# A state space layer: two states per scan, with a zero-decay column between them

## The chip, the cores and the metric

The kernel runs on one core of a Trainium2 chip. The metric is device time in microseconds of one execution. A core has five engines with a queue each, which meet only at semaphores: TensorE (PE in the profile; its weight loads are PEld), VectorE (DVE), ScalarE (ACT), GpSimd (POOL) and SyncE (SP), which issues the transfers here. Data lies in SBUF, matmul results and some scratch in PSUM, which has eight banks of 512 fp32 values per partition.

## The reference

Two layers follow each other on an image x of 4 x 384 x 64 x 64, each with a group norm before it and a residual after it. The first is a state space layer over the 4096 positions of an image, with 768 inner channels and 16 states a channel; the second is a windowed attention with 7 x 7 windows. Only the first is touched by the change. Its core, with the projections before it left out:

```python
dt = jax.nn.softplus(jnp.einsum('blr,dr->bld', dt, dt_w) + dt_b)
A = -jnp.exp(A_log)
def step(h, inp):
    dt_t, B_t, C_t, x_t = inp
    dA = jnp.exp(dt_t[:, :, None] * A[None])
    dBx = (dt_t * x_t)[:, :, None] * B_t[:, None, :]
    h = dA * h + dBx
    y_t = jnp.einsum('bdn,bn->bd', h, C_t)
    return (h, y_t)
```

So for each channel d and state n there is a recurrence over positions, h = dA h + dt x B, and the output of a position is the sum over n of C h. Everything is fp32.

## The kernel before

An image's 4096 positions are cut into 16 chunks of T = 256; with four images this makes 64 steps. A step has 768 channels as 6 tiles of 128 partitions (index d), and the 16 states as 4 groups of 4 (index g). The pair (d, g) is numbered m = 4d + g, 0 to 23. Each m has two half groups of two states, so a step has 48 half groups. These are the kernel's clock: a plan lists for each of the 48 slots of a step what else is emitted there, and all engines run their queues in the order of emission.

For one m the work is:

- `decay` (ScalarE): for each of the two states of a half group, dA = exp(dt x A) over 256 positions, written to a PSUM tile `da` of one bank; two such tiles take turns. The decays of the next half group are emitted ahead of the scans of this one.
- `driven`: dt x B for four states at once, 1024 elements, written to an SBUF tile `db` (six in turn). For 9 of the 24 m's GpSimd does it, from `dtx` in SBUF; for 15 VectorE does it, from a copy of dtx in a PSUM bank of its own, `dtx_ps`. The table `driven_at` (L692) gives the slot and the engine.
- `dt_x` (GpSimd) makes dtx = dt times x once per d, and `dt_x_copied` (ScalarE) copies it to PSUM two slots later.
- `scans` (VectorE): the recurrence, one instruction per state over 256 positions, from `da`, `db` and a start value that is a pointer to the state kept from the chunk before (a constant 0 in an image's first chunk). The result goes to `hs` (five in turn).
- `with_c` (GpSimd): copies the last position of four states to `state`, then multiplies hs by C in place.
- `summed` (TensorE): eight transposing matmuls add the four states into PSUM; `turn` copies the sum out with ScalarE (`ys`), turns it back with TensorE and lets VectorE multiply by the gate.

Between these the plan places the work for the next steps: the projections and the convolution (TensorE, evicted by ScalarE with a bias), a burst of Silu activations with two table loads, the softplus in three parts (`softplus`: matmul, four Abs/Relu parts, Exp and an addition, Ln on ScalarE; three corrections on VectorE), the norm of the step after next, the output projection of the step before, and once per 24 slots statistics of the next image. Tiles of the pool `ps0` ("mm" in the profile), four PSUM banks in turn, hold all the matmul results.

The loads of B and C, broadcast to 128 partitions, and the image tiles are issued by SyncE. Semaphores are placed by a layer that follows tiles: an instruction waits for the earlier instructions that wrote or read the same tile or, in PSUM, the same tile's banks.

The line numbers in the profile are those of the kernel before. L96 is the helper through which all activations go.

Of the kernel before, what the change touches and what calls it, by code (L numbers as in the profile page):

```python
# [8 lines left out]
F32 = mybir.dt.float32  # L9
# [13 lines left out]
NG = 4  # L23
# [25 lines left out]
def two_layers(  # L49
# [151 lines left out]

    state = w0.tile([P, ND, NS], F32, name="state")
    xb = w0.tile([P, ND, KC - 1 + T], F32, name="xb")
# [67 lines left out]
    def layer0(x1s, mvs, gms1):  # L271

        with ExitStack() as es:
            es.enter_context(tc.manual_schedule(engines=in_step))
            ps_a = es.enter_context(tc.tile_pool(name="ps_a", bufs=2, space=PSUM))
            ps_x = es.enter_context(tc.tile_pool(name="ps_x", bufs=1, space=PSUM))
            ps_y = es.enter_context(tc.tile_pool(name="ps_y", bufs=1, space=PSUM))
            ps = es.enter_context(tc.tile_pool(name="ps0", bufs=4, space=PSUM))
            bc = es.enter_context(tc.tile_pool(name="bc", bufs=4))
            w1 = es.enter_context(tc.tile_pool(name="w1", bufs=1))  # L280
            w2 = es.enter_context(tc.tile_pool(name="w2", bufs=2))
            gms, gbs, st1s = {}, {}, {}
            dtx_ps = ps_x.tile([P, 2, T], F32, name="dtx_ps")

# [17 lines left out]
            def next_batch(b, at):  # L302
# [15 lines left out]
                for n in range(NJ * NXT):  # L318
                    t, j = divmod(n, NJ)
                    at(24 * n + 14, lambda t=t, j=j: load(t, j))  # L320
                    at(24 * n + 26, lambda t=t, j=j: nc.vector.bn_stats(st[:, j, t, :], h["x"]))
                end = 24 * NJ * NXT + 24
# [7 lines left out]
            def normed(I, h, at):  # L330
# [26 lines left out]
                def with_row(key, op):  # L357
                    nc.vector.tensor_tensor(
                        h["xn"], h["xn"], h[key][:, 0:1, :].broadcast_to([P, NJ, T]), op
                    )  # L360
# [10 lines left out]
                at(22, by_group)  # L371
                at(24, lambda: mean("xn", "mu"))
                at(26, lambda: with_row("mu", ALU.subtract))
                at(30, square)
                at(31, lambda: mean("sq", "var"))
                at(34, root)
                at(35, lambda: with_row("var", ALU.mult))

# [20 lines left out]
            def prepared(I, h, at):  # L399
# [21 lines left out]

                at(-11, kept)
                for p, (x, c, z) in enumerate((
                    ((-10, -9, -6), (1, 2, 5), (9, 10, 13)),
                    ((-6, -5, -2), (3, 4, 7), (12, 13, 16)),
                    ((-4, -3, 0), (7, 8, 11), (15, 16, 19)),
                )):
# [50 lines left out]

                at(26, burst)
                at(28, lambda: x_proj((0, 1, 2)))  # L480
                at(29, lambda: x_proj((3, 4, 5)))
                at(32, rows)

# [45 lines left out]

                for q, first in enumerate((34, 36, 46)):  # L530
                    softplus(q, first)

            dbs, das = {}, {}

# [7 lines left out]
            def dt_x_copied(d, h):  # L542
                nc.scalar.copy(dtx_ps[:, d % 2, :], h["dtx"][d])

            def driven(I, m, h, eng):

                d, g = divmod(m, NS // NG)
                db = w2.tile([P, NG, T], F32, tag="db", name=f"db_{I}_{m}", bufs=6)
                dtx = dtx_ps[:, d % 2, :] if eng is nc.vector else h["dtx"][d]
                eng.tensor_tensor(  # L550
                    db, dtx.unsqueeze(1).broadcast_to([P, NG, T]), h["B"][g], ALU.mult
                )
                dbs[I, m] = db

            def decay(I, m, half, h):

                d, g = divmod(m, NS // NG)
                da = ps_a.tile([P, 2, T], F32, tag="da", name="da")
                for k in range(2):
                    n = g * NG + 2 * half + k  # L560
                    act(da[:, k, :], h["dt"][d // 2][:, d % 2, :], AF.Exp, scale=nega[:, d, n : n + 1])
                das[I, m, half] = da

            def scans(I, m, half, hs):

                d, g = divmod(m, NS // NG)
                da = das.pop((I, m, half))
                for k in range(2):
                    j = 2 * half + k
                    n = g * NG + j  # L570
                    nc.vector.tensor_tensor_scan(  # L571
                        hs[:, j, :], da[:, k, :], dbs[I, m][:, j, :],
                        state[:, d, n : n + 1] if I % NCHUNK else 0.0,
                        ALU.mult, ALU.add,
                    )

            def with_c(I, m, h, hs):

                d, g = divmod(m, NS // NG)
                nc.gpsimd.tensor_copy(state[:, d, g * NG : (g + 1) * NG], hs[:, :, T - 1])  # L580
                nc.gpsimd.tensor_tensor(hs, hs, h["C"][g], ALU.mult)  # L581

            def summed(I, m, h, hs):
# [6 lines left out]
                for k in range(NG):  # L590
                    first = g == 0 and k == 0
                    last = g == NS // NG - 1 and k == NG - 1
                    for half in range(2):
                        nc.tensor.matmul(  # L594
                            y[:, d % 2, half, :], hs[:, k, half * P : (half + 1) * P], ident,
                            is_transpose=True, start=(first and half == 0 and d % 2 == 0),
                            stop=(last and half == 1 and d % 2 == 1), skip_group_check=True,
                        )

            def turn(I, p, h, at, s):  # L600

# [25 lines left out]
                at(s, out)  # L627
                at(s + 1, back)
                at(s + 4, gated)

            def out_proj(I, h, at):
# [37 lines left out]
                at(10, reload)  # L669
                for n, slot in enumerate((17, 18, 19, 20, 22, 23)):  # L670
                    m, part = divmod(n, 2)
                    at(slot, lambda m=m, part=part: tile_part(m, range(3 * part, 3 * part + 3)))
                at(26, lambda: residual(0, 2))
                at(28, lambda: residual(2, 1))
                at(30, stats)
# [8 lines left out]
            def slot_of(I):  # L684
# [9 lines left out]
                (12, 0), (15, 1), (17, 1), (18, 1), (20, 0), (22, 1), (24, 0), (26, 1),  # L694
                (26, 1), (26, 1), (30, 0), (33, 1), (36, 0), (39, 1), (40, 0), (43, 1),
            )
            dt_x_at = (-5, 2, 10, 18, 22, 34)

            for I in range(STEPS):
                h = steps[I]  # L700
                for p in range(ND // 2):
                    turn(I, p, h, slot_of(I), (p + 1) * (SLOTS // 3) + 4)
                out_proj(I, h, slot_of(I + 1))
# [5 lines left out]
                for m, (slot, vector) in enumerate(driven_at):  # L709
                    eng = nc.vector if vector else nc.gpsimd  # L710
                    slot_of(I)(slot, lambda I=I, m=m, h=h, eng=eng: driven(I, m, h, eng))
                if I % NCHUNK == 0 and I + NCHUNK < STEPS:
# [26 lines left out]
            for n in range(STEPS * M):  # L739
                I, m = divmod(n, M)  # L740
                hs = w2.tile([P, NG, T], F32, tag="hs", name=f"hs_{I}_{m}", bufs=5)
                for half in range(2):
# [422 lines left out]
```

## Time and profile before

| what | value |
|---|---|
| median of 7 runs | 8370.22 us (8360.2 to 8372.64) |
| the profiled execution's own time | 8370.22 us |
| its span in the profile | 8368.5 us |
| state space layer, first to last scan | 114 to 6021 us |
| attention layer | the rest, about 2300 us |
| VectorE / GpSimd / TensorE / ScalarE busy, whole span | 87 / 85 / 87 / 69% |
| the same from 2000 to 3000 us | 98 / 92 / 84 / 79% |
| granted TensorE clock there | 0.90 |

How to read it. A line of the groups of instructions names the source line, the engine, the operation, out<-in by the program's names, the shapes and the count; then, after the colon or bar, the busy time in us and the mean of one instruction in ns; then how long the engine had been idle before these instructions and which work ended most of that. A line of the timeline gives the start in us, the length in us, engine, line and operation, how many equal instructions follow each other (x4), and in brackets an idle time and what ended it. Instructions of one engine can overlap at their ends, so the distance between starts is what an instruction costs its engine.

### The profile page before, as it was taken

The numbers are of one execution on the slowest core, as the hardware profiler recorded it, in microseconds if no ns is written. First come the engines' busy times: TensorE is split into PE (matmuls) and PEld (weight loads), VectorE is DVE, ScalarE is ACT, GpSimd is POOL, SyncE is SP. The second block draws the span as 40 slices with busy tenths as digits, with TensorE's granted clock in tenths as the row PEclk, the third lists the DMA queues.
The fourth block names the chain that finished last, engine by engine and source line by source line (L and its number), as shares of the span: only waits on it lengthen the run. The fifth ranks groups of instructions, "written<-read, shape, count | busy, mean of one in ns | idle before, by whom it ended". The sixth has DMA issues, their size and how long they took to land. (4 is left out here: it accounts for less than half of the span.)

```text
span 8368.5 us, 139186 instructions
## 1 busy us (share of the span) xinstructions
PE 7250.8 (87%) x45882; PEld 5492.5 (66%) x45882; DVE 7312.5 (87%) x13300; ACT 5810.4 (69%) x13758; POOL 7092.7 (85%) x5719
## 2 busy tenths in 40 slices
PE   7888888888888888888888888888699999999999
PEld 5676677777667667676777677766555555555555
DVE  5999999999999999999999999999766666666666
ACT  5777777777777777777777777777545455455455
POOL 4999999999999999999999999999767677677677
PEclk9988898889888998999899889889799999999999
DMA  3112211121122112211211121112223233233232
GB/s 112 59 61 66 75 58 54 64 72 58 63 67 71 53 60 68 69 58 65 71 59 54 57 70 55 54 61 66 70 85 87 75 96 88 75 92 85 84 86 65
DMA packets 327504, 583.06 MB, mean 70 GB/s; under 512 B 62940, under 2 KB 211180, under 8 KB 326660
## 3 DMA queue, kind: packets, MB, share of 16 engines
q1 hardware_dynamic: 326788, 574.17, 22.1%
q8 instruction: 370, 6.06, 0.3%
q14 instruction: 346, 2.83, 0.1%
HBM read 471.49 MB, written 84.73 MB: 66 GB/s over the span
## 5 line engine op out<-in xcount | busy, mean ns | idle before, releaser
L571 DVE TENSOR_TENSOR_SCAN hs<-da,state,db 128x256 f32<-128x256 f32 x5760 | 3856.5, 729 | 88.8 <-ACT da L96 64.6
L96 ACT ACTIVATE da<-dt,nega 128x256 f32<-128x256 f32 x6144 | 2918.0, 477 | 1211.4 <-DVE hs L571 1105.3
L581 POOL TENSOR_TENSOR hs<-hs,C 128x1024 f32<-128x1024 f32 x1536 | 3621.5, 2358 | 123.9 <-POOL state L580 0.4
L594 PE MATMUL y<-ident,hs 128*128 128x128 f32 x12288 | 1773.3, 296 | 910.0 <-POOL hs L581 907.7
L594 PEld LDWEIGHTS y<-ident,hs 128*128 128x128 f32 x12288 | 1538.0, 153 | 1213.2 <-POOL hs L581 1107.2
L941 POOL TENSOR_SCALAR sg<-sg,rsum 128x308 f32<-128x308 f32 x1536 | 1619.9, 1073 | 643.8 <-DVE rsum L939 641.8
L550 POOL TENSOR_TENSOR db<-dtx,B 128x1024 f32<-128x1024 f32 x576 | 1360.2, 2361 | 0.1
L550 DVE TENSOR_TENSOR db<-dtx_ps,B 128x1024 f32<-128x1024 f32 x960 | 1142.5, 1201 | 0.0
L382 PE MATMUL mm_ps<-xn,w_in 128*128 128x256 f32 x4608 | 1125.2, 391 | 11.0 <-DVE yg L624 9.1
L96 ACT ACTIVATE sg<-sg,mx 128x308 f32<-128x308 f32 x1536 | 828.6, 541 | 252.0 <-DVE mx L926 232.9
L926 DVE CUSTOM_DVE_ANT_0 sg<-lg_ps,bias 128x308 f32<-128x308 f32 x1536 | 643.1, 475 | 384.8 <-PE lg_ps L920 384.8
L382 PEld LDWEIGHTS mm_ps<-xn,w_in 128*128 128x128 f32 x4608 | 872.6, 197 | 119.9 <-DVE yg L624 9.6
L389 PE MATMUL mm_ps<-xb,dcv 128*128 128x256 f32 x3072 | 782.3, 408 | 0.0
L389 PEld LDWEIGHTS mm_ps<-xb,dcv 128*128 128x128 f32 x3072 | 616.2, 208 | 87.6 <-issue 0.3
L969 ACT COPY tb<-pt_ps 88x512 f32<-88x512 f32 x384 | 221.8, 578 | 625.1 <-PE pt_ps L965 625.1
L580 POOL COPY state<-hs 128x4 f32<-128x4 f32 x1536 | 288.6, 188 | 342.5 <-DVE hs L571 336.0
L639 PE MATMUL mm_ps<-yg,w_out 128*128 128x256 f32 x2304 | 538.1, 384 | 0.0
L956 DVE COPY ta<-pt_ps 110x512 f32<-110x512 f32 x768 | 492.4, 683 | 23.2 <-PE pt_ps L951 23.2
L639 PEld LDWEIGHTS mm_ps<-yg,w_out 128*128 128x128 f32 x2304 | 437.9, 194 | 58.1
L951 PE MATMUL pt_ps<-ident,sg 128*110 128x128 f32 x3072 | 417.7, 279 | 0.8 <-POOL sg L941 0.8
L951 PEld LDWEIGHTS pt_ps<-ident,sg 128*110 128x110 f32 x3072 | 322.7, 133 | 77.9 <-issue 48.4
L824 PE MATMUL mm_ps<-xn,w_qkv 128*128 128x512 f32 (+2 forms) x612 | 279.9, 595 | 60.4 <-DVE xn L811 53.2
(141 smaller groups left out, 9148.2 us busy)
## 6 DMA issues: line engine op xcount, KB each, us to landing
B<-bcrows SPq DMA_DIRECT2D x256, 512.0 KB
C<-bcrows SPq DMA_DIRECT2D x256, 512.0 KB
vw<-vd SPq DMA_DIRECT2D x1792, 33.0 KB
xr<-x SPq DMA_DIRECT2D x28, 1056.0 KB
vd<-v SPq DMA_DIRECT2D x280, 96.0 KB
xi<-in_x_dram SPq DMA_DIRECT2D x64, 384.0 KB
xo<-in_x_dram SPq DMA_DIRECT2D x64, 384.0 KB
x<-xo SPq DMA_DIRECT2D x64, 384.0 KB
```

What stands on the lines that cost most here:

```text
L96: ins = nc.scalar.activation(o, i, func, **kw)
L382: nc.tensor.matmul(pb[:, k, :], w_in[:, j, m * P : (m + 1) * P], xn[:, j, :], start=(j == 0), stop=(j == NJ - 1),)
L389: nc.tensor.matmul(pb[:, k, :], dcv[:, d, c, :], xb[:, d, c : c + T], start=(c == 0), stop=(c == KC - 1),)
L550: eng.tensor_tensor(db, dtx.unsqueeze(1).broadcast_to([P, NG, T]), h["B"][g], ALU.mult)
L571: nc.vector.tensor_tensor_scan(hs[:, j, :], da[:, k, :], dbs[I, m][:, j, :], state[:, d, n : n + 1] if I % NCHUNK else 0.0, ALU.mult, ALU.add,
L581: nc.gpsimd.tensor_tensor(hs, hs, h["C"][g], ALU.mult)
L594: nc.tensor.matmul(y[:, d % 2, half, :], hs[:, k, half * P : (half + 1) * P], ident, is_transpose=True, start=(first and half == 0 and d % ...
L639: nc.tensor.matmul(h["po", first][:, m - first, :], w_out[:, d, m * P : (m + 1) * P], h["yg"][d // 2][:, d % 2, :], start=(d == 0), stop=( ...
L926: nc.vector.tensor_tensor_reduce(sg[:, hh, :], lg[:, :NK], bias[:, 4 * m + hh, :], -1.0, BIG, ALU.add, ALU.min, mx[:, hh : hh + 1],)
L941: nc.gpsimd.tensor_scalar(sg[:, hh, :], sg[:, hh, :], rs[:, hh : hh + 1], None, ALU.mult)
L951: nc.tensor.transpose(pt[: KN[c], col : col + P], sg[:, 2 * pair + hh, KOFF[c] : KOFF[c] + KN[c]], ident,)
L956: nc.vector.tensor_copy(t[: KN[0], :, :].rearrange("p a q -> p (a q)"), pt[: KN[0], :])
```

## The change

Two states share one scan. The scan runs over 513 elements: 256 positions of the first state, one column, 256 positions of the second. In the column the decay is 0 and the addend is the second state's kept value, so that the recurrence arrives at exactly that value there, whatever the first state ended with, and goes on with the second state. A step has 48 scans in place of 96.

What goes with it:

- `da` and `dtx_ps` become two PSUM tiles `pair_0` and `pair_1` of 1024 values, two banks each. Each holds one dtx (256 values), then 256 decays, the zero column and 256 decays. Half group 0 of any m uses pair_0, half group 1 pair_1; dtx of an even d is in pair_0, of an odd d in pair_1. The zero columns are written once, before the loop.
- `db` and `hs` become tiles of 2 x 513 per partition. The products reach the four states by a four-dimensional access (`states`).
- `opened` is new: a ScalarE copy of two elements writes the two columns of `db` from the kept states, two slots ahead of `driven`. In an image's first chunk it copies zeros.
- `state` becomes 24 tiles of 4 values in place of one of 96.
- The pool of matmul banks has three in place of four.
- In the plan the projections, the convolution, the norm, the softplus, the B and C rows, the output projection and the statistics move by one to several slots; `driven` of m = 16 and 17 moves from slot 26 to 27; the third part of the softplus starts at 43 in place of 46.

```diff
-    state = w0.tile([P, ND, NS], F32, name="state")
+    state = [
+        [w0.tile([P, NG], F32, name=f"state_{d}_{g}") for g in range(NS // NG)] for d in range(ND)
+    ]
...
-            ps_a = es.enter_context(tc.tile_pool(name="ps_a", bufs=2, space=PSUM))
-            ps_x = es.enter_context(tc.tile_pool(name="ps_x", bufs=1, space=PSUM))
+            ps_a = es.enter_context(tc.tile_pool(name="ps_a", bufs=1, space=PSUM))
             ps_y = es.enter_context(tc.tile_pool(name="ps_y", bufs=1, space=PSUM))
-            ps = es.enter_context(tc.tile_pool(name="ps0", bufs=4, space=PSUM))
+            ps = es.enter_context(tc.tile_pool(name="ps0", bufs=3, space=PSUM))
...
-            dtx_ps = ps_x.tile([P, 2, T], F32, name="dtx_ps")
+            pairs = [ps_a.tile([P, 4 * T], F32, name=f"pair_{k}") for k in range(2)]
+            dtx_ps = [t[:, 0:T] for t in pairs]
+            da_ps = [t[:, T : 3 * T + 1] for t in pairs]
+            for t in da_ps:
+                nc.vector.memset(t[:, T : T + 1], 0.0)
...
-                at(-11, kept)
+                at(-4, kept)
                 for p, (x, c, z) in enumerate((
-                    ((-10, -9, -6), (1, 2, 5), (9, 10, 13)),
-                    ((-6, -5, -2), (3, 4, 7), (12, 13, 16)),
-                    ((-4, -3, 0), (7, 8, 11), (15, 16, 19)),
+                    ((-3, -2, 1), (4, 5, 8), (11, 12, 15)),
+                    ((-1, 0, 3), (6, 7, 10), (13, 14, 17)),
+                    ((3, 4, 7), (9, 10, 13), (15, 16, 19)),
                 )):
...
-                at(26, burst)
-                at(28, lambda: x_proj((0, 1, 2)))
-                at(29, lambda: x_proj((3, 4, 5)))
-                at(32, rows)
+                at(27, burst)
+                at(29, lambda: x_proj((0, 1, 2)))
+                at(30, lambda: x_proj((3, 4, 5)))
+                at(33, rows)
...
-                for q, first in enumerate((34, 36, 46)):
+                for q, first in enumerate((35, 37, 43)):
                     softplus(q, first)
...
             def dt_x_copied(d, h):
-                nc.scalar.copy(dtx_ps[:, d % 2, :], h["dtx"][d])
+                nc.scalar.copy(dtx_ps[d % 2], h["dtx"][d])
+
+            def states(t):
+                return bass.AP(
+                    t.tensor, t.offset, [t.ap[0], [2 * T + 1, 2], [T + 1, 2], [1, T]]
+                )
+
+            def opened(I, m):
+                d, g = divmod(m, NS // NG)
+                db = dbs[I, m] = w2.tile(
+                    [P, 2, 2 * T + 1], F32, tag="db", name=f"db_{I}_{m}", bufs=6
+                )
+                kept = state[d][g].rearrange("p (a k) -> p a k", k=2)
+                nc.scalar.copy(db[:, :, T : T + 1], kept[:, :, 1:2] if I % NCHUNK else zeros)

             def driven(I, m, h, eng):
-                db = w2.tile([P, NG, T], F32, tag="db", name=f"db_{I}_{m}", bufs=6)
-                dtx = dtx_ps[:, d % 2, :] if eng is nc.vector else h["dtx"][d]
+                db = dbs[I, m]
+                dtx = dtx_ps[d % 2] if eng is nc.vector else h["dtx"][d]
                 eng.tensor_tensor(
-                    db, dtx.unsqueeze(1).broadcast_to([P, NG, T]), h["B"][g], ALU.mult
+                    states(db), dtx.unsqueeze(1).unsqueeze(1).broadcast_to([P, 2, 2, T]),
+                    h["B"][g].rearrange("p (a k) t -> p a k t", k=2), ALU.mult,
                 )
...
             def decay(I, m, half, h):
-                da = ps_a.tile([P, 2, T], F32, tag="da", name="da")
                 for k in range(2):
                     n = g * NG + 2 * half + k
-                    act(da[:, k, :], h["dt"][d // 2][:, d % 2, :], AF.Exp, scale=nega[:, d, n : n + 1])
+                    act(
+                        da_ps[half][:, k * (T + 1) : k * (T + 1) + T],
+                        h["dt"][d // 2][:, d % 2, :], AF.Exp, scale=nega[:, d, n : n + 1],
+                    )

             def scans(I, m, half, hs):
-                for k in range(2):
-                    j = 2 * half + k
-                    n = g * NG + j
-                    nc.vector.tensor_tensor_scan(
-                        hs[:, j, :], da[:, k, :], dbs[I, m][:, j, :],
-                        state[:, d, n : n + 1] if I % NCHUNK else 0.0,
-                        ALU.mult, ALU.add,
-                    )
+                nc.vector.tensor_tensor_scan(
+                    hs[:, half, :], da_ps[half], dbs[I, m][:, half, :],
+                    state[d][g][:, 2 * half : 2 * half + 1] if I % NCHUNK else 0.0,
+                    ALU.mult, ALU.add,
+                )

             def with_c(I, m, h, hs):
-                nc.gpsimd.tensor_copy(state[:, d, g * NG : (g + 1) * NG], hs[:, :, T - 1])
-                nc.gpsimd.tensor_tensor(hs, hs, h["C"][g], ALU.mult)
+                by_state = states(hs)
+                nc.gpsimd.tensor_copy(
+                    state[d][g].rearrange("p (a k) -> p a k", k=2), by_state[:, :, :, T - 1]
+                )
+                nc.gpsimd.tensor_tensor(
+                    by_state, by_state, h["C"][g].rearrange("p (a k) t -> p a k t", k=2), ALU.mult
+                )
...
                 for m, (slot, vector) in enumerate(driven_at):
                     eng = nc.vector if vector else nc.gpsimd
+                    slot_of(I)(slot - 2, lambda I=I, m=m: opened(I, m))
                     slot_of(I)(slot, lambda I=I, m=m, h=h, eng=eng: driven(I, m, h, eng))
```

## Prediction, made before the changed kernel was run

> **What bounds the kernel now.** Three views, in this order. First the busy times by stage: the change touches only the state space layer, which by the kernel's scan rows runs from 114 to 6021 us, 64 steps of 92.3 us. A stretch inside it:
>
> ```profile
> core 0: us, PE busy (x) PEld busy (x) DVE busy (x) ACT busy (x) POOL busy (x), PEclk, DMA share, GB/s
> 2000.00:3000.00 1000.00, 841.23 (x4424) 696.49 (x4424) 983.71 (x1431) 787.40 (x1721) 918.55 (x691) 0.90 0.20 65
> ```
>
> VectorE is busy 98% of the time, GpSimd 92%, ScalarE 79%. So VectorE sets the pace, with GpSimd 6% behind. Second, the groups of instructions:
>
> ```profile
> L571 DVE TENSOR_TENSOR_SCAN hs<-da,state,db 128x256 f32<-128x256 f32 x5760 | 3856.5, 729 | 88.8 <-ACT da L96 64.6
> L96 ACT ACTIVATE da<-dt,nega 128x256 f32<-128x256 f32 x6144 | 2918.0, 477 | 1211.4 <-DVE hs L571 1105.3
> L581 POOL TENSOR_TENSOR hs<-hs,C 128x1024 f32<-128x1024 f32 x1536 | 3621.5, 2358 | 123.9 <-POOL state L580 0.4
> L550 POOL TENSOR_TENSOR db<-dtx,B 128x1024 f32<-128x1024 f32 x576 | 1360.2, 2361 | 0.1
> L550 DVE TENSOR_TENSOR db<-dtx_ps,B 128x1024 f32<-128x1024 f32 x960 | 1142.5, 1201 | 0.0
> ```
>
> The scans wait little; ScalarE waits 1105 us for them before the next decays. ScalarE's slack is what the change will spend. Third, the timeline, because a row's mean hides that instructions overlap:
>
> ```profile
> 2999.64 0.67 DVE L624 TENSOR_TENSOR yg<-mm_ps,sz 128x512 f32<-128x512 f32 x1
> 2999.76 0.99 ACT L96 ACTIVATE da<-dt,nega 128x256 f32<-128x256 f32 x2 [1.07 <-DVE hs L571]
> 3000.23 2.67 DVE L571 TENSOR_TENSOR_SCAN hs<-da,state,db 128x256 f32<-128x256 f32 x4
> ...
> 3002.69 0.18 POOL L580 COPY state<-hs 128x4 f32<-128x4 f32 x1
> 3002.81 1.20 DVE L550 TENSOR_TENSOR db<-dtx_ps,B 128x1024 f32<-128x1024 f32 x1
> ...
> 3002.95 2.35 POOL L581 TENSOR_TENSOR hs<-hs,C 128x1024 f32<-128x1024 f32 x1
> ...
> 3003.92 6.75 DVE L571 TENSOR_TENSOR_SCAN hs<-da,state,db 128x256 f32<-128x256 f32 x10
> ...
> 3005.26 0.73 POOL L537 TENSOR_TENSOR dtx<-dt,xc 128x256 f32<-128x256 f32 x1
> ...
> 3005.94 0.19 POOL L580 COPY state<-hs 128x4 f32<-128x4 f32 x1
> ```
>
> ```profile
> 1585.88 5.24 DVE L571 TENSOR_TENSOR_SCAN hs<-da,state,db 128x256 f32<-128x256 f32 x8
> 1591.03 1.20 DVE L550 TENSOR_TENSOR db<-dtx_ps,B 128x1024 f32<-128x1024 f32 x1
> 1592.15 2.42 DVE L571 TENSOR_TENSOR_SCAN hs<-da,db 128x256 f32<-128x256 f32 x4
> 1594.49 1.20 DVE L550 TENSOR_TENSOR db<-dtx_ps,B 128x1024 f32<-128x1024 f32 x1
> ```
>
> From start to start a scan holds VectorE (1591.03 - 1585.88)/8 = 0.643 us, not 0.729; with a constant start value, (1594.49 - 1592.15)/4 = 0.585; the 1024-element product 1.115, the 512-element one 0.59. The last 0.083 us of an operation lie under the next.
>
> **The change part by part.** A *slot* is one half group: 48 a step.
>
> *One scan of 513 for two of 256.* No scan that long is in the trace. The two products give (1.115 - 0.59)/512 = 1.03 ns per element and 0.06 us fixed. The scan without a state pointer costs as much as 512 such elements, so 2.07 ns per element and 0.06 fixed; the pointer adds 0.06. For 513: 1.06 + 0.06 + 0.06 = 1.18 us against 1.286. Saved: 0.109 x 48 = 5.2 us a step. Bounds: everything scales with length (1.286, nothing saved), or the pointer is free too (1.12, 8 us saved). I take 1.18; two kinds of row agree on it.
>
> *Zero column, state column.* 24 ScalarE copies of two elements a step. Copies of 512 and 256 take 0.578 and 0.370: 0.16 at no length, less about 0.06 of overlap; the 32x1 activation takes 0.20 to 0.24. Between 0.10 and 0.20; I take 0.12, 2.9 us a step on an engine with slack, counted inside the walk below. The two memsets run once.
>
> *Strided access on GpSimd and VectorE.* Runs stay 256 long. GpSimd's copies of short strided rows (128x72, 0.26 us) are near its four-element copy (0.19), so I take no cost; upper bound 10% of 33 x 2.31 us = 7.6 us a step. GpSimd by starts: 24 x (0.26 + 2.31) + 9 x 2.31 + 6 x 0.68 = 86.6 us a step. It covers up to 92.3, so 5.7 us more on it stay hidden.
>
> *Moved slots, three banks instead of four, states in 24 tiles.* Each projection keeps its three slots between matmul and eviction; TensorE is 84% busy and off the path (ScalarE waited 27 us for projections in the whole run). The B loads are queued behind the release of old B tiles, not behind the moved row store. Nothing, with 0 to 0.5 us a step as bounds.
>
> *The shared tile.* This decides. dtx now lies in the tile that holds the decays, and the dependencies go by tile: a dt x B product on VectorE waits for the newest decay pair in its tile, a decay pair waits for a product that reads its tile, a dtx copy waits for the scan of its tile or holds up the next one. Before, dtx had a bank of its own and products filled the time in which ScalarE was late. The Trainium skill (PSUM — Partial Sum Buffer, section "PSUM bank collisions raise a hardware error") says that two engines in one bank must be kept apart even at different addresses, ScalarE and VectorE included; so these waits cannot be dropped while the bank is shared. No row here shows a collision; with the waits the sum is the one below, without them the first rival's.
>
> I price it by walking both queues slot by slot. Scan k starts when its decays are ready and VectorE is free, and ends 1.26 us later; decays for k+2 start 0.035 after that end and after ScalarE's other work, and take 0.99. ScalarE's other work, by starts: two evictions 0.71, four softplus parts 1.42, exp and add 1.18, log 0.48, ys copy 0.48, dtx copy 0.31, Silu burst 5.7.
>
> Example, with the scan of slot 45 at 0: decays for 47 run 1.30 to 2.29; four softplus parts to 3.65; decays for 48 to 4.64. Scans 46 and 47 issue at 1.18 and 2.35, VectorE is free at 3.53; the product of slot 47 reads tile 0, where the decays for 48 go, and waits to 4.67: 1.14 us lost. Before, it ran at 3.5 and covered them.
>
> The other places, likewise: slot 5 (ys, dtx copy) 0.63; 10 (evictions after decays that waited for a product) 0.55; 14 and 15 (dtx copy behind its scan, evictions) 0.95; 21 (ys and dtx copy in the tile scanned next) 1.22; 24 (group norm) 0.19; 37 (dtx copy) 0.48; 40 to 43 (softplus) 1.31. With slot 47: 6.5 us a step. The same walk over the kernel before gives 0.21 + 0.29 + 0.92 = 1.4; its trace shows 1.6 at the same three places, one being
>
> ```profile
> 3055.33 1.39 DVE L571 TENSOR_TENSOR_SCAN hs<-da,state,db 128x256 f32<-128x256 f32 x2 [0.85 <-ACT da L96]
> ```
>
> (0.85 idle and 0.08 hidden). So the walk is good to 0.2 us where it can be tested. ScalarE's mid-step wait for the fourth dtx,
>
> ```profile
> 3027.51 0.38 ACT L543 COPY dtx_ps<-dtx 128x256 f32<-128x256 f32 x1 [0.68 <-POOL dtx L537]
> ```
>
> then delays decays with nothing over them: some 0.25 more. Sum per step: -5.2 + (6.5 - 1.4) + 0.25 + 0.2 for what the walk missed before = +0.3 us, x 64 = +20 us. The profiled execution took 8370.22 us (span 8368.5), which is also the median: 8390 us.
>
> A check inside the trace: in the first step of batch 2, from 1592.15 on, the 96 scans are 0.058 us cheaper, 5.6 us in all. From its first scan to the next step's it takes 90.4 us, where steps with the same other work take 92.6. Of 5.6 us saved on VectorE 2.2 arrive, even without a shared tile.
>
> **Rivals.**
> *Faster:* the waits through the shared tile cost little, because products and copies fall where VectorE or ScalarE waits anyway. The walk without them loses 3.7 us a step: -5.2 + 2.3 + 0.25 = -2.6, x 64 = -170, 8200 us; half-way 8290. For it: ScalarE's 1105 us of waiting. Against: the list above. It decides once the stalls stay under 5.9 us a step.
> *The scan is not cheaper:* 513 elements at 1.286. The waits shrink as VectorE is slower (walk: 4.5), so +3.1 + 0.25 a step, 8580 us. For it: only that no row shows a long scan; against: both fits.
> *GpSimd becomes the bound:* four-dimensional access 10% dearer: 86.6 + 7.6 = 94.2 plus its waits, about +2.5 a step, 8530 us; from about 7% on it decides. For it: GpSimd at 92%; against: the strided copies.
>
> **How the numbers follow.** Chances: the balance 0.55 (own range 8340 to 8440), faster rival 0.30, dear scan 0.08, GpSimd 0.07. The bound of what can be told from no change is 0.2%, 17 us. Of the balance, half lies above 8387, under 0.3 within, under 0.2 below; of the faster rival nearly all lies below. Faster 0.35, same 0.18, slower 0.47. The range 8240 to 8490 leaves out the far end of the faster case and most of the two dear ones.
>
> **What would show it.** A scan row of 128x513 near 1.26 us, 1.18 from start to start (wrong: over 1.3). VectorE's busy share down from 98% to 92 or 93%, its waits for decays up from 82 us to several hundred, with the product group waiting too, which it did not. The two-element copies near 0.2 us. GpSimd's rows unchanged at 2.36 us. If VectorE shows few waits and steps of 90 us, the shared tile was overpriced; if GpSimd never waits for a scan, GpSimd has become the bound.

## The result, and the profile after

The changed kernel takes 8389.01 us (median of 14 runs, 8386.3 to 8393.86), the kernel before 8369.19 us (34 runs): a ratio of 1.0026, 95% interval 1.0019 to 1.0033. The forecast was 8390. The profiled execution has a span of 8390.2 us, against 8368.5 before, and the scans end at 6042.9 us against 6021.3: all of the difference lies in the state space layer.

Busy times of the same stretch, 2000 to 3000 us, in the changed kernel:

```profile
core 0: us, PE busy (x) PEld busy (x) DVE busy (x) ACT busy (x) POOL busy (x), PEclk, DMA share, GB/s
2000.00:3000.00 1000.00, 842.25 (x4400) 699.69 (x4398) 935.53 (x911) 804.88 (x1972) 895.41 (x691) 0.89 0.20 65
```

VectorE is busy 93.5% of the time in place of 98%, and a step is as long as before: what the scans gave up has become idle time. GpSimd is less busy, not more. The groups of instructions say where the free time lies. Line numbers are now those of each run's own kernel; here L594 is the scan, L575 the product for `db`, L552 the copy of dt x into PSUM, L568 the column copy, L604 and L607 GpSimd's copy of the last position and its product with C:

```profile
L594 DVE TENSOR_TENSOR_SCAN hs<-pair,state,db 128x513 f32<-128x513 f32 x2880 | 3570.1, 1272 | 278.7 <-ACT pair L96 135.9 <-ACT pair L552 126.7 <-POOL db L575 0.5
L575 DVE TENSOR_TENSOR db<-pair,B 128x1024 f32<-128x1024 f32 x960 | 1153.0, 1207 | 68.3 <-ACT pair L96 68.3
...
L568 ACT COPY db<-state 128x2 f32<-128x2 f32 x1440 | 253.4, 180 | 0.0
...
L607 POOL TENSOR_TENSOR hs<-hs,C 128x1024 f32<-128x1024 f32 x1536 | 3488.6, 2271 | 124.1 <-POOL state L604 0.6
...
L575 POOL TENSOR_TENSOR db<-dtx,B 128x1024 f32<-128x1024 f32 x576 | 1367.3, 2374 | 0.4 <-DMA B<-bcrows 0.4
```

Scans now wait 279 us, about half of it for decays (L96) and half for dt x copies (L552). Before, they waited 89. The products, which never waited, wait 68 us, all of it for decays in the tile that they read. The list of waits from 1000 to 5000 us shows the other side of the same tile (us in all, how many, the longest):

```profile
...
ACT pair L96 <- DVE hs L594: 317.0, 536, 3.2
POOL state L604 <- DVE hs L594: 304.9, 138, 3.4
ACT pair L96 <- DVE db L575: 303.2, 172, 3.7
DVE hs L594 <- ACT pair L96: 98.2, 188, 1.0
DVE hs L594 <- ACT pair L552: 90.5, 126, 1.2
...
DVE db L575 <- ACT pair L96: 46.9, 43, 1.4
...
DVE yg L653 <- PE mm_ps L646: 13.9, 3, 4.6
```

ScalarE waits 303 us for VectorE's products (L575), a wait that the kernel before did not have. GpSimd still waits for scans (L604). The last line is rare but long; it comes back below. The timeline at the end of a step shows the example that the prediction worked out, slot 45 to 47:

```profile
2242.99 3.63 DVE L594 TENSOR_TENSOR_SCAN hs<-pair,state,db 128x513 f32<-128x513 f32 x3
2243.61 0.38 ACT L552 COPY pair<-dtx 128x256 f32<-128x256 f32 x1
...
2244.30 0.99 ACT L96 ACTIVATE pair<-dt,nega 128x256 f32<-128x256 f32 x2 [0.19 <-DVE hs L594]
...
2245.22 0.45 ACT L96 ACTIVATE spe<-mm_ps,dtb 128x256 f32<-128x256 f32 x1
...
2246.65 1.00 ACT L96 ACTIVATE pair<-dt,nega 128x256 f32<-128x256 f32 x2
...
2247.68 1.23 DVE L575 TENSOR_TENSOR db<-pair,B 128x1024 f32<-128x1024 f32 x1 [1.07 <-ACT pair L96]
```

Three scans in 3.63 us, so (3.63 - 1.27)/2 = 1.18 us from start to start. The product cannot start before the decays for slot 48, issued behind the softplus parts, are in: 1.07 us idle, and with the 0.08 hidden under the scan's end 1.15 lost; the prediction had 1.14.

By steps (first scan to first scan) the difference is made up so. Of the 63 distances, three (steps 12, 28, 44) are longer by 4.2 us each, 12.6 in all; the four first steps of an image by 2.2 each, 8.6; the other 56 together are 1.6 us shorter: ordinary ones take 92.38 in place of 92.59 us, those without statistics of the next image 92.26 in place of 91.98. The first scan starts 2.6 us later, which was not followed up. 12.6 + 8.6 - 1.6 + 2.6 makes 22, the difference of the spans.

### The profile page after: what moved, and what is told of

The parts are those of the page before. It is cut to its first block, busy times and chain, and to the rows that moved or that the text cites. A ratio compares the mean times of both kernels' runs of the same rounds, so it can differ in the third digit from the quotient of the medians.

```text
span 8390.2 us, 137885 instructions
## 1 busy us (share of the span) xinstructions
PE 7260.8 (87%) x45882; PEld 5505.3 (66%) x45882; DVE 7051.4 (84%) x10231; ACT 5933.9 (71%) x15294; POOL 6959.7 (83%) x5719
## 4 chain that ended last, share of the span: by engine, by line
PE 27%; POOL 22%; ACT 19%; DVE 18%; issue 13%; DMA 0%; SPq 0%; POOLq 0%; DVEq 0%; ACTq 0%
POOL hs L607 13%; DVE hs L594 10%; ACT pair L96 9%; POOL db L575 6%; DVE db L575 4%; PE pt_ps L981 4%; PE lg_ps L950 3%; PE mm_ps L854 3%; PE mm_ps L1034 3%; PE mm_ps L887 3%; PE mm_ps L917 3%; PE pv_ps L1007 3%; PE pt_ps L995 2%; ACT spe L96 2%; POOL dtx L546 2%
## 5 line engine op out<-in xcount | busy, mean ns | idle before, releaser
L594 DVE TENSOR_TENSOR_SCAN hs<-pair,state,db 128x513 f32<-128x513 f32 x2880 | 3570.1, 1272 | 278.7 <-ACT pair L96 135.9
L96 ACT ACTIVATE pair<-dt,nega 128x256 f32<-128x256 f32 x6144 | 2922.0, 477 | 1052.6 <-DVE hs L594 477.5
L607 POOL TENSOR_TENSOR hs<-hs,C 128x1024 f32<-128x1024 f32 x1536 | 3488.6, 2271 | 124.1 <-POOL state L604 0.6
L623 PE MATMUL y<-ident,hs 128*128 128x128 f32 x12288 | 1858.0, 304 | 731.4 <-POOL hs L607 698.1
L623 PEld LDWEIGHTS y<-ident,hs 128*128 128x128 f32 x12288 | 1598.2, 157 | 1082.2 <-POOL hs L607 918.8
L575 POOL TENSOR_TENSOR db<-dtx,B 128x1024 f32<-128x1024 f32 x576 | 1367.3, 2374 | 0.4 <-DMA B<-bcrows 0.4
L389 PE MATMUL mm_ps<-xn,w_in 128*128 128x256 f32 x4608 | 1180.1, 402 | 91.1 <-ACT xb L96 61.8
L575 DVE TENSOR_TENSOR db<-pair,B 128x1024 f32<-128x1024 f32 x960 | 1153.0, 1207 | 68.3 <-ACT pair L96 68.3
L96 ACT ACTIVATE sg<-sg,mx 128x308 f32<-128x308 f32 x1536 | 828.6, 541 | 251.7 <-DVE mx L956 233.2
L396 PE MATMUL mm_ps<-xb,dcv 128*128 128x256 f32 x3072 | 745.2, 390 | 111.6 <-DVE dt L527 107.6
L396 PEld LDWEIGHTS mm_ps<-xb,dcv 128*128 128x128 f32 x3072 | 578.8, 193 | 214.0 <-DVE dt L527 129.6
L604 POOL COPY state<-hs 128x4 f32<-128x4 f32 x1536 | 290.3, 189 | 478.9 <-DVE hs L594 451.1
L546 POOL TENSOR_TENSOR dtx<-dt,xc 128x256 f32<-128x256 f32 x384 | 282.9, 737 | 121.4 <-DVE dt L527 121.4
```

Source lines behind the costliest of these rows:

```text
L96: ins = nc.scalar.activation(o, i, func, **kw)
L389: nc.tensor.matmul(pb[:, k, :], w_in[:, j, m * P : (m + 1) * P], xn[:, j, :], start=(j == 0), stop=(j == NJ - 1),)
L396: nc.tensor.matmul(pb[:, k, :], dcv[:, d, c, :], xb[:, d, c : c + T], start=(c == 0), stop=(c == KC - 1),)
L575: eng.tensor_tensor(states(db), dtx.unsqueeze(1).unsqueeze(1).broadcast_to([P, 2, 2, T]), h["B"][g].rearrange("p (a k) t -> p a k t", k=2) ...
L594: nc.vector.tensor_tensor_scan(hs[:, half, :], da_ps[half], dbs[I, m][:, half, :], state[d][g][:, 2 * half : 2 * half + 1] if I % NCHUNK e ...
L607: nc.gpsimd.tensor_tensor(by_state, by_state, h["C"][g].rearrange("p (a k) t -> p a k t", k=2), ALU.mult)
```

## Experiments

The theory: the long scan saves what was forecast, some 5.1 us a step, and waits through the tile that now holds both decays and dt x give it back. The rivals: the rebuilt plan or the third matmul bank cost the time, or the scan saves nothing. Step lengths are ordinary steps' medians; a *wait* is how much the distance between two starts on VectorE exceeds its usual one, summed over an ordinary step; what is taken as usual moves such a sum by some 0.2 us. The *ring* in the expectations is the circle in which ScalarE, VectorE and GpSimd wait for each other's results.

**Two scans again, without column copies; tiles and plan kept.**

```diff
-                nc.scalar.copy(db[:, :, T : T + 1], kept[:, :, 1:2] if I % NCHUNK else zeros)
...
-                nc.vector.tensor_tensor_scan(
-                    hs[:, half, :], da_ps[half], dbs[I, m][:, half, :],
...
+                for k in range(2):
+                    at, j = k * (T + 1), 2 * half + k
+                    nc.vector.tensor_tensor_scan(
+                        hs[:, half, at : at + T], da_ps[half][:, at : at + T],
...
```

> The changed kernel with its tiles and its plan, but two scans of 256 elements a half group again and no column copies. Theory (VectorE with ScalarE's decays sets the pace, and a scan of 513 saves 5.2 us a step of which the waits take part): +5.2 for the scans, -2.3 because a slower VectorE waits less, about +2.9 us a step, 8575 us. Rival (GpSimd or TensorE binds, the scan's saving reaches nothing): within 30 us of 8389.

Measured: 8560.64 us, ratio 1.0228 (1.0212 to 1.0243). Tiles and plan without the long scan cost 2.3%; the long scan then brings 172 us back. A step takes 95.11 us with 4.19 us of waits; with the long scan 92.38 with 6.54. So the long scan with its column copies saves 2.73 us a step: 5.1 on the scans, less 2.36 of waits that are added. That they come because VectorE reaches ScalarE's work sooner is the reading that fits, not shown apart.

**The shared tile taken away, at two scans.** Decays get a bank each, the two dt x share a third. 513 columns do not fit a bank, so this was tried with two scans only, and what the sharing costs at the long scan was not measured by itself.

```diff
-            pairs = [ps_a.tile([P, 4 * T], F32, name=f"pair_{k}") for k in range(2)]
-            dtx_ps = [t[:, 0:T] for t in pairs]
-            da_ps = [t[:, T : 3 * T + 1] for t in pairs]
...
+            da_ps = [ps_a.tile([P, 2 * T], F32, name=f"da_{k}") for k in range(2)]
+            x_ps = ps_a.tile([P, 2, T], F32, name="x_ps")
+            dtx_ps = [x_ps[:, k] for k in range(2)]
```

> The run with two scans of 256 again (8560.6 us, after's plan of slots, three matmul banks), with one thing changed: the decays have a bank of their own each and the two dt x tiles share a third, so no tile holds both. Theory (the shared pair tile gives rise to the waits that took the scan's gain back): VectorE's products no longer wait for the newest decay pair and decays no longer wait for products; by the same arithmetic as in the prediction, at two scans a slot, a step is 92.3 us without the shared tile and 94.6 with it, so about 147 us less: 8415. Rival (the rebuilt plan of slots or the three banks for matmuls are what cost, not the sharing): 8560 within 20. If both have a part, the time lies between, and the stalls left say where.

Measured: 8454.41 us, ratio 1.0106 (1.0091 to 1.0122): 106 us less. What VectorE waits for from 1000 to 5000 us, first with the shared tile, then without:

```profile
DVE hs L595 <- ACT pair L552: 60.5, 85, 1.1
DVE hs L595 <- ACT pair L96: 46.4, 129, 1.2
DVE db L574 <- ACT pair L96: 37.6, 42, 1.2
```

```profile
DVE hs L593 <- ACT da L96: 87.7, 184, 1.7
DVE hs L593 <- POOL hs L607: 14.3, 54, 0.5
```

The waits for the dt x copies and of the products are gone. Those for decays have grown; it fits that VectorE now comes earlier to the places where ScalarE is late anyway. A step takes 93.57 us, with 2.6 us of waits, so the tile is worth 1.54 us a step, where the arithmetic gave 2.3 (94.6 less 92.3). One thing was left untried: in the pair tiles dt x shares its bank of 512 values with the first state's decays alone, since the second state's begin in the next bank. Yet the product of slot 47 above starts only when both decays are in.

**Four matmul banks.** The kernel with dt x in a bank of its own, `bufs=3` to `bufs=4` in the pool ps0.

> The run with dt x in a bank of its own and two scans of 256 (8454.4 us), with four matmul banks in place of three and nothing else changed. Theory: a bank short is dear only where the group norm of the next image takes one; steps 12, 28 and 44, which took 8.3 us more than an ordinary one, fall to some 2 us more, as in the kernel before: 6 x 3 = 19 us less, 8435, and ordinary steps stay at 93.6 us. Rival (three banks also hold up ordinary steps): ordinary steps fall by 0.3 us or more, 8415 or less.

Measured: 8444.53 us, ratio 1.0093 (1.0078 to 1.0108): 10 us less. Ordinary steps stay (93.54); steps 12, 28 and 44 fall from 101.87 to 97.44 us, 13.3 together. That is where a bank short is dear. The changed kernel's timeline in step 12:

```profile
1301.63 1.28 DVE L594 TENSOR_TENSOR_SCAN hs<-pair,state,db 128x513 f32<-128x513 f32 x1 [0.75 <-ACT pair L96]
...
1303.43 1.01 ACT L96 ACTIVATE pair<-dt,nega 128x256 f32<-128x256 f32 x2
1304.38 0.24 ACT L96 ACTIVATE grs_a<-psv_a,eps 32x1 f32<-32x1 f32 x1
...
1304.67 0.69 PE L641 MATMUL mm_ps<-ident,ys 128*128 128x128 f32 x2 [7.34 <-ACT grs_a L96]
```

The group norm of the next image has a bank until ScalarE, behind softplus and decays, has taken its variance out (`psv_a`). TensorE waits 7.34 us for that bank to turn a sum back, and VectorE's gating (`yg`) waits 4.6 us for TensorE.

With the three runs an ordinary step adds up: 92.59 before; 93.54 with the new plan and layouts, four banks and dt x apart (plan and layouts were not tried one without the other); 93.57 with three banks; 95.11 with the shared tile; 92.38 with the long scan.

**The norm's parts where a bank is free.**

```diff
-                for n, part in enumerate(group_norm(b + 1, mv)):
-                    at(end + 2 + 3 * n, part)
+                for slot, part in zip((3, 5, 51, 53, 54, 55, 57, 58, 58), group_norm(b + 1, mv)):
+                    at(end + slot, part)
```

> The changed kernel with one thing moved: the nine parts of the next image's group norm (which take matmul banks) sit in slots in which one of the three banks is free, no longer at slots 26 to 50 of the step 12 of an image. Theory (with three banks the gate's matmuls wait for a bank there, 4.7 us at slot 41 in three steps): steps 12, 28 and 44 fall from 98.8 to about 94.5 us, 3 x 4.2 = 13 us, 8376 us. Rival (those steps are long because of the small VectorE operations): 8389 us.

Measured: 8384.59 us, ratio 1.0017 (1.0008 to 1.0027), an interval that overlaps the changed kernel's; 4.4 us less by the medians, 8.7 by the profiled spans, where 13 were expected. Step 12 falls from 98.76 to 93.00, step 13 rises from 92.35 to 95.00: by steps 12 to 18 together 3 us saved, three times.

**dt x from SBUF, so that nothing is shared and nothing copied.** Done in the changed kernel and, as a control, in the kernel before.

```diff
-                dtx = dtx_ps[d % 2] if eng is nc.vector else h["dtx"][d]
+                dtx = h["dtx"][d]
...
-                    slot_of(I)(slot + 2, lambda d=d, h=h: dt_x_copied(d, h))
```

> The changed kernel, but the products on VectorE read dtx from SBUF, so the six dtx copies of a step are gone and nothing but decays lies in the pair tiles. Theory (the waits through the shared tile give the saving back): stalls fall from 6.5 to about 3.3 us a step, in all some 3.2 us x 64 = 200 us, 8180 us. Rival 1 (GpSimd or the three matmul banks bind the changed kernel): at most 20 us, above 8365 us. Rival 2 (two SBUF inputs make the VectorE product or GpSimd dearer): the product row rises from 1.207 us, or GpSimd's rows from 2.27 and 2.37; at 1.4 us for the product nothing is gained, 8390 us.

> The kernel before with the same edit, as a control: dtx had a bank of its own there, so only six ScalarE copies a step go, which lay in its slack, and one wait of 0.7 us of ScalarE for GpSimd. Theory: unchanged products, 8370 us, at most 20 us faster. If two SBUF inputs are dear, slower by 15 x the product's rise x 64 (100 us for 0.1 us).

Measured: 8906.96 us, ratio 1.0643 (1.0627 to 1.0659), and 9107.79, ratio 1.0883 (1.0867 to 1.0899). The groups of the first:

```profile
L575 DVE TENSOR_TENSOR db<-dtx,B 128x1024 f32<-128x1024 f32 x960 | 1726.8, 1804 | 0.0
...
L575 POOL TENSOR_TENSOR db<-dtx,B 128x1024 f32<-128x1024 f32 x576 | 1604.4, 2785 | 0.4 <-ACT db L568 0.4
L604 POOL COPY state<-hs 128x4 f32<-128x4 f32 x1536 | 758.5, 494 | 80.3 <-DVE hs L594 80.2
```

The same product takes 1.80 us in place of 1.21, GpSimd's takes 2.79 in place of 2.37, and its four-element copy 0.49 in place of 0.19; in the control the three take 1.94, 2.57 and 0.60. The second SBUF input alone is not what is dear: in the first run the ten products that ran while GpSimd stood idle took 1.21 us each, and others up to 3.25. The Trainium skill (GPSIMD Engine Reference, section "1. Specifications") says that GpSimd shares its SBUF interfaces with VectorE and contends with VectorE instructions of two SBUF inputs; these rows agree. So the copies in PSUM pay for themselves. On the shared tile this says nothing, since the contention is dearer.

**Copies later; then two products earlier as well.** For odd d the copy goes to slots 5, 21, 37, where the next scan does not read its tile; in the second run m = 1 and m = 2 move too (the first two lines of the diff; the first run has the copies alone).

```diff
-                (-4, 0), (-1, 1), (1, 1), (2, 1), (4, 0), (7, 1), (8, 0), (10, 1),
+                (-4, 0), (-2, 1), (0, 1), (2, 1), (4, 0), (7, 1), (8, 0), (10, 1),
...
-                    slot_of(I)(slot + 2, lambda d=d, h=h: dt_x_copied(d, h))
+                    slot_of(I)(slot + (2, 3, 2, 3, 2, 3)[d], lambda d=d, h=h: dt_x_copied(d, h))
```

> The changed kernel with the copies of dt x into PSUM of d = 1, 3 and 5 a slot later, in slots 5, 21 and 37 in place of 4, 20 and 36, where the tile that they write is the one whose scan has just been read and not the one that the next scan reads. Theory of the shared tile: the 0.61, 1.19 and 0.34 us that scans wait for these copies fall; some 0.9 us of other waits come in their place in the next slots; net 0.6 to 0.7 us a step, 40 to 45 us: 8346. Rival (ScalarE is simply late there and the copy is the last thing seen): within 10 us of 8389.

> The run before this one, and with it VectorE's products of m = 1 and m = 2 a slot earlier (46 and 0 in place of 47 and 1), where the dt x that they read is not in the tile of the newest decay pair. Theory of the shared tile: the 1.15 us that the product waits in slot 47 is gone and nothing comes for it; a step is 1.8 us under that of the changed kernel, 116 us: 8273, under the kernel before by 96. Rival (the waits move on to the next scan, since ScalarE is the ring's slower side): 8346, as with the copies alone.

Measured: 8383.02 us, ratio 1.0019 (1.0010 to 1.0028), and 8319.38 us, ratio 0.9944 (0.9931 to 0.9956). VectorE's waits in the first, then in the second:

```profile
DVE hs L594 <- ACT pair L96: 164.7, 379, 1.2
DVE db L575 <- ACT pair L96: 47.3, 44, 1.4
```

```profile
DVE hs L594 <- ACT pair L96: 166.5, 383, 1.1
DVE yg L653 <- PE mm_ps L646: 13.9, 3, 4.6
```

The 90.5 us of waits for copies went, and 66 of them came back as waits for decays, besides smaller gaps that the list puts down to nothing: the scans around those slots wait for ScalarE in any case, and the step became 0.12 us shorter, not 0.6. The 47 us of the products went for good: 0.97 us a step. So the first forecast fails towards its rival, and the second's own part, 1.15 us in slot 47, nearly holds. The second kernel is faster than the kernel before.

**Column copies twice.**

```diff
-                nc.scalar.copy(db[:, :, T : T + 1], kept[:, :, 1:2] if I % NCHUNK else zeros)
+                for _ in range(2):
+                    nc.scalar.copy(db[:, :, T : T + 1], kept[:, :, 1:2] if I % NCHUNK else zeros)
```

> The changed kernel with each column copy of ScalarE issued twice. ScalarE gets 24 more copies a step of 0.08 us each from start to start, 1.9 us. Theory: most of it falls in ScalarE's free time; what lies ahead of a decay pair that a scan waits for delays the scan: 0.2 to 0.4 us a step, 13 to 26 us: 8402 to 8415. Rival (ScalarE's order decides every slot): all of it, 1.9 us a step, 8513. Rival (hidden whole): within 8 us of 8389.

Measured: 8475.11 us, ratio 1.0128 (1.0114 to 1.0142), 86 us over the changed kernel; 1.23 us a step. The size was wrong because the second copy costs more than the first. A lone copy in the changed kernel, and a pair here:

```profile
2195.61 0.19 ACT L568 COPY db<-state 128x2 f32<-128x2 f32 x1
2195.70 0.99 ACT L96 ACTIVATE pair<-dt,nega 128x256 f32<-128x256 f32 x2
```

```profile
2279.41 0.40 ACT L569 COPY db<-state 128x2 f32<-128x2 f32 x2
```

The second copy starts some 0.21 us after the first, where a lone copy mostly holds ScalarE 0.08 us. Both write the same place; whether that is the reason was not tried. The waits grew by 0.23 us before each of the scans of slots 10, 40 and 43, and by about 0.1 before those of 1, 15, 22, 24 and 26: at those places ScalarE's time is VectorE's time, elsewhere the copies are free. What a single copy costs, this run does not give.

**All products placed by the arithmetic.** With 0.16 us for a column copy the walk gives the measured waits of three kernels. That number is fitted to them: from start to start the trace has 0.08. With it, thirteen of the fifteen products (the expectation says eleven, a miscount) and two copies were placed anew. The second run also moves the norm, as above.

```diff
-                (-4, 0), (-1, 1), (1, 1), (2, 1), (4, 0), (7, 1), (8, 0), (10, 1),
-                (12, 0), (15, 1), (17, 1), (18, 1), (20, 0), (22, 1), (24, 0), (26, 1),
-                (27, 1), (27, 1), (30, 0), (33, 1), (36, 0), (39, 1), (40, 0), (43, 1),
+                (-4, 0), (-3, 1), (-1, 1), (3, 1), (4, 0), (6, 1), (8, 0), (9, 1),
+                (12, 0), (13, 1), (18, 1), (19, 1), (20, 0), (23, 1), (24, 0), (27, 1),
+                (27, 1), (28, 1), (30, 0), (33, 1), (36, 0), (38, 1), (40, 0), (41, 1),
...
-                    slot_of(I)(slot + 2, lambda d=d, h=h: dt_x_copied(d, h))
+                    slot_of(I)(slot + (2, 2, 3, 5, 2, 2)[d], lambda d=d, h=h: dt_x_copied(d, h))
```

> The changed kernel with eleven of VectorE's fifteen products and two of the copies of dt x in other slots, chosen by the prediction's arithmetic for the two engines' order, with 0.16 us for a column copy (at which that arithmetic gives the waits measured in the changed kernel, with the copies later, and with the first products moved: 6.6, 6.2 and 5.3 us by it, 6.54, 6.33 and 5.27 measured). Theory (the waits come from where products and copies stand in the tile that both engines share, and the plan can avoid them): waits of 2.4 us a step in place of 6.5, 4.1 x 64 = 262 us: 8125. Rival (GpSimd, busy 0.895 of these steps, some 82.7 us of each, holds the ring back as soon as the step gets near 88): a step of 88 to 90 us with waits for GpSimd in it, 8170 to 8240. Rival (waits through the shared tile come back wherever products stand): 8319, as with the first products moved alone.

> The run before this one, with the nine parts of the next image's group norm in slots where one of the three matmul banks is free, as in the run on that part alone (which took 4.4 us off). Theory: 4 to 13 us less than the run before this one, three steps by 1.5 to 4.2 us each. Rival (the wait that they make lies beside others): the same within 3 us.

Measured: 8241.2 us, ratio 0.9853 (0.9836 to 0.9869), and 8229.23 us, ratio 0.9837 (0.9822 to 0.9852). Steps of 90.1 us with 4.2 us of waits. The arithmetic had forgotten one kind of wait, a product in the very slot of its copy, and the list of waits of the first run names it:

```profile
DVE db L575 <- ACT pair L552: 75.7, 88, 1.4
DVE hs L594 <- ACT pair L96: 45.9, 70, 0.9
```

The norm's move took 12 us here by the medians, 10.4 by the spans: step 12 from 96.51 to 90.61 us, step 13 up by 2.6.

**Copies back, products kept.** Against the last run:

```diff
-                (12, 0), (13, 1), (18, 1), (19, 1), (20, 0), (23, 1), (24, 0), (27, 1),
-                (27, 1), (28, 1), (30, 0), (33, 1), (36, 0), (38, 1), (40, 0), (41, 1),
+                (12, 0), (13, 1), (18, 1), (19, 1), (20, 0), (22, 1), (24, 0), (27, 1),
+                (27, 1), (27, 1), (30, 0), (33, 1), (36, 0), (38, 1), (40, 0), (41, 1),
...
-                    slot_of(I)(slot + (2, 2, 3, 5, 2, 2)[d], lambda d=d, h=h: dt_x_copied(d, h))
+                    slot_of(I)(slot + 2, lambda d=d, h=h: dt_x_copied(d, h))
```

> The kernel of the run with the whole plan and the norm moved (8229.2 us), with all copies of dt x back where the changed kernel has them (12 and 20 in place of 13 and 23 for d = 2 and 3) and the product of m = 13 in slot 22, of m = 17 in 27: only products, and the norm's parts, stand elsewhere than in the changed kernel. In that run the products of slots 13 and 23 waited 0.43 and 1.51 us for the copy issued in their own slot; the arithmetic had left that wait out, and with it gives 4.0 us of waits there (4.2 measured) and 2.5 to 2.9 here. Theory: 1.1 to 1.4 us a step less, 70 to 91 us: 8140 to 8160. Rival (GpSimd, busy 0.92 of the run before, holds the ring from here on): 8180 to 8229, with waits for GpSimd's products in the place of those for copies.

Measured: 8228.82 us, ratio 0.9835 (0.9822 to 0.9849): nothing gained. The 1.5 us of the product in slot 23 and 0.3 us before the scan of slot 16 are gone; 0.85 us more before the scan of slot 26, 0.45 in slot 13, 0.3 before 17 and 0.2 before 24 came for them. The timeline before the scan of slot 26:

```profile
2146.31 0.74 POOL L546 TENSOR_TENSOR dtx<-dt,xc 128x256 f32<-128x256 f32 x1
...
2147.08 0.38 ACT L552 COPY pair<-dtx 128x256 f32<-128x256 f32 x1 [1.56 <-POOL dtx L546]
2147.26 2.27 POOL L607 TENSOR_TENSOR hs<-hs,C 128x1024 f32<-128x1024 f32 x1
2147.49 0.99 ACT L96 ACTIVATE pair<-dt,nega 128x256 f32<-128x256 f32 x2
...
2148.52 1.29 DVE L594 TENSOR_TENSOR_SCAN hs<-pair,state,db 128x513 f32<-128x513 f32 x1 [0.86 <-ACT pair L96]
```

In this part of the step GpSimd's instructions follow each other without a pause that the trace shows, so it makes dt x late; ScalarE's copy waits 1.56 us for it, the decays queue behind the copy, and the scan waits for the decays. Over 1000 to 5000 us these waits of ScalarE are

```profile
ACT pair L552 <- POOL dtx L546: 106.9, 84, 1.6
```

against 24.0 us in the run before and 45.6 in the changed kernel. They stand at two of the six dt x: 1.58 us for d = 4, before the scan of slot 26, and 0.93 for d = 2, before the product of slot 13. So the rival was right on the outcome, and GpSimd (busy 92%) holds the others up at these two places, some 1.8 of the 4 us of waits in a step, though not through its products, as expected, but through short dt x that queue between its long operations. At slot 41, where the decays stand behind the softplus, VectorE still waits some 0.9 us, much as in the changed kernel. Placing GpSimd's own work anew was not tried.

## Why the prediction was right

- *The scan*: 1.18 us from start to start (1.176 to 1.20 where nothing is waited for), as worked out from the two rows; the rival of the dear scan falls with it.
- *The signs*: the scan's row (1272 ns), the column copies (180 ns) and VectorE's busy share came as named. Of the 347 us that scans and products wait, 127 are for dt x copies and not for decays.
- *The shared tile*: waits of 6.54 us a step against 6.5. By place, forecast and measured: slot 5 0.63 and 0.61; 10 0.55 and 0.50; 14 and 15 0.95 and 1.14; 21 1.22 and 1.20; 24 0.19 and 0.21; 37 0.48 and 0.34; 40 to 43 1.31 and 1.19; 47 1.14 and 1.15. Ahead of 14 and 15 ScalarE's copy for d = 2 waits 0.99 us for GpSimd, which the walk did not have. The faster rival's point of decision, 5.9 us, was passed. But the 6.5 us are not the tile's alone. Before, 1.6 us were waited; of the 4.9 that were added the runs put 1.54 to the tile (at two scans), 0.95 to plan and layouts and 2.36 to the cheaper scan. The walk had the sum right and the shares less so: it gave the tile 2.3 us at two scans (6.5 - 3.7 = 2.8 at the long one), and without the tile a step of two scans took 93.57 us where it had 92.3.
- *The added 0.25 us for ScalarE's wait for the fourth dt x* (d = 4, slot 24) was too much: ScalarE still waits 0.44 us there, but VectorE has no wait over 0.05 us at slots 25 and 26. The 0.2 for what the walk missed before had the wrong sign: with the 1.6 us that the trace showed in place of the walk's 1.4, the waits added are 6.5 - 1.6 = 4.9, and the sum would have been -0.3, or about nothing with the 0.25. With both additions, ordinary steps were forecast at +0.3 us; they came out at -0.21, or +0.28 where no statistics run.
- *"Moved slots, three banks instead of four"* was taken as nothing, with 0.5 us a step as the upper bound, and failed: plan and layouts make 0.95 us a step at two scans. Three banks cost 13.3 us in three steps by the run with four. The argument looked at the projections' slots and at TensorE's busy share and overlooked the one user that holds a bank for long, the norm of the next image.
- *The first steps of an image* were not priced apart. Scans with a constant start were 0.058 us cheaper 96 times a step; now 0.05 cheaper 48 times, so there the long scan saves less: 8.6 us in four steps.
- *Column copies*: a lone one holds ScalarE 0.08 us, not 0.12.
- *GpSimd as the bound* falls: its rows hardly changed (2271 and 2374 ns against 2358 and 2361), and it waits for scans.
- *The chances* do not quite follow from their parts: half of 0.55 with 0.08 and 0.07 makes 0.43 for slower, not 0.47.

So the nearly exact total is partly luck. The scan's saving and the sum of the waits were right to 0.1 us a step; the 56 plain steps came out 18 us better than 0.3 x 56 (-1.6 in place of +16.8), and the norm, the first steps and the start, 24 us together, made up for it.

## What to carry to other kernels

When a faster instruction is bought by putting two tensors into one tile, walk both engines' queues slot by slot with start-to-start times, because the price is which wait ends last in each slot, not the busy shares; a wait that is seen last may only hide a late engine, so that removing it (the copies here) brings little where moving the work that truly waits (the products) brings much. When a pool of banks shrinks, look for the rare user that holds a bank longest, not at the average. And then place the work anew for the new dependencies: the change as given cost 0.26%, the same scan with the products and the norm's parts placed for it saves 1.6%. The kernel before was not placed anew. All the 1.6 us of waits in each of its 64 steps would be worth some 100 us, about 8267 us, an estimate from its trace; the changed kernel reached 8229.

## What the runs showed of the hardware that was not expected

GpSimd's in-place product with C takes 2271 ns on the rows of 2 x 513 and 2358 ns on rows of 4 x 256 before; with two scans on the new rows it is 2273, so it goes with the layout and not with the scan. Its product for db did not gain (2374 against 2361). Why is open.

Two copies of two elements that write the same place start 0.21 us apart on ScalarE, while what follows a single one starts 0.08 us after it, when it has nothing to wait for.
